# One mending branch in place of two ahead of the last unit's readings, in a mixture-of-experts tail

## The chip, the cores and the metric

The kernel runs on one core of a Trainium2 chip. The metric is device time in microseconds of one execution; lower is better. All numbers below come from runs of this program and from one profiled execution of it.

## What is computed

The program is a two-layer decoder on 8 sequences of 512 tokens and 256 channels, in float32. Only the end of the second layer matters here, the mixture of experts. Cut to that:

```python
tokens = hidden_states.reshape(-1, H)                  # 4096 x 256
topk_idx, topk_w = _route(tokens, ...)                 # 4 of 32 experts for each token
hidden_vals = silu(tokens @ gate_w) * (tokens @ up_w)  # for each expert
expert_out = hidden_vals @ down_w
mixed = (expert_out[topk_idx] * topk_w).sum(1)         # the 4 chosen experts' rows, weighted, added up
out = x + mixed + shared
```

## The kernel before, in words

The 4096 tokens are cut into 8 units of 512 tokens. A unit has 512 x 4 = 2048 assignments of a token to an expert, that is 16 tiles of 128. Routing sorts the assignments by expert and unit into a list in DRAM, `rows`, in pages of 128; each expert's share begins on a page of its own, so up to 32 pages (NE) are partly empty. In all there may be up to 160 pages (NS), and the program works through the first 136 (SURE, L31) without asking. How many pages are in use is known only on the chip.

**The main loop** is `pages_of(0, SURE, between)` (L1634, called at L1685), in an order written out by hand. For each page: SyncE (SP) reads the page (`fetch`, L1528), TensorE turns and multiplies it, VectorE (DVE) and ScalarE (ACT) evacuate, ACT weighs the result (L1574), and GpSimd (POOL) scatters the 128 result rows to their tokens' places in DRAM, `results`, by an indirect transfer (L944).

**The readings.** When a unit's pages are certainly done, its four tiles of 128 tokens are read back: `gather` (L1579) is a transfer of 512 KB on SP's queue into a buffer `z` of [128, 4, 256]; `add` (L1595) is three DVE instructions (L1602 one of 128x512, L1604 two of 128x256) that add the 4 rows of each token to `x`; `put` writes the sums to the output (L1612, two tiles at once on SP's queue, in the main loop; L1614, one tile on ACT's queue, after it). `finish` (L1619) puts these for units 0 to 6 between the pages.

**What may go wrong, and is mended.** A unit's readings are placed as if its pages ended at NE + 16 for each unit. Router sums say whether that was so. `experts` (L1352, run once before the main loop) makes two numbers in `used`: the rows in use, and how many of the first seven units ended later than `through` (L1373, L1374). After the main loop each of the five engines loads both numbers into registers (L1671) and branches on them:

- `rest(SURE)` (L1663): if more than 136 pages are in use, eight more pages, and within that branch the next eight, up to 160.
- `complete(range(7))` under `unready > 0` (L1702): if one of the first seven units was read too early, all of them are read, added and put once more.
- `complete([7])` (L1706), always: the last unit's four gathers, and per tile three additions and a put.

So the last unit's readings stand behind both branches.

**What a branch is in the built program.** Transfers on SP's and ACT's queues are counted in eight counters in turn (here HW0 to HW7), POOL's in eight others (SW0 to SW7), and each engine has a counter for its own instructions. After a branch the counters must stand the same whichever way it went. So the way around has, on each engine, one instruction for each counter that the engine's part of the branch would have moved: it waits until the counter has reached what was to come before the branch, and then adds what the branch would have added. On SP that is eight such instructions, in the order HW0 to HW7; on DVE and ACT one; on POOL four waits and one increment. Behind the second branch the first gather waits besides for the counters as the way around left them.

The last things SP does before the branches are two puts of unit 5 and two of unit 6 (L1612). The last put of unit 6 and the DVE addition it waits for were placed by the builder behind the first branch and ahead of the second.

Of the kernel before, what the change touches and what calls it, by code (L numbers as in the profile page):

```python
# [12 lines left out]
F32 = mybir.dt.float32  # L13
# [3 lines left out]
ALU = mybir.AluOpType  # L17
# [4 lines left out]
P = 128  # L22
B, S, H = 8, 512, 256
NT = S // P
# [6 lines left out]
SURE = 136  # L31
# [5 lines left out]
NE = 32  # L37
TOPK = 4
# [768 lines left out]
def _halves(x, u):  # L807

    h, p = divmod(u, B // 2)
    return [x[2 * p + r][:, 2 * h + t, :] for r in range(2) for t in range(2)]  # L810
# [54 lines left out]
def _l1(nc, tc, a, x, out, ident, mhalf, rows, results, filled, inputs, early):  # L865
# [12 lines left out]
    U = B  # L878
    seen = lambda u: 4 if u % 4 < 2 else 8
    with ExitStack() as ctx:  # L880
        pool = lambda name, bufs, **kw: ctx.enter_context(tc.tile_pool(name=name, bufs=bufs, **kw))
        routing, attention = ExitStack(), ExitStack()
        wp = routing.enter_context(tc.tile_pool(name="m_w", bufs=1, side="right"))
# [6 lines left out]
        vec = _Recorded(nc.vector)  # L890
# [13 lines left out]
            shared.append((gate, up, down))  # L904
        consts = {}
        for name, shape in (
            ("router_bias", [NE]), ("before", [16]), ("through", [U - 1])
        ):
            consts[name] = wp.tile([P, *shape], F32, tag=name, name=name)
            nc.sync.dma_start(consts[name], a[name].partition_broadcast(P))  # L910
        for name, width in (("earlier", P), ("pages", 2)):
            consts[name] = wp.tile([P, width], F32, tag=name, name=name)
            nc.sync.dma_start(consts[name], a[name])
        rb, before, earlier, pages, through = (
            consts[n] for n in ("router_bias", "before", "earlier", "pages", "through")
        )
# [15 lines left out]
        bounds = wp.tile([P, U, NE], F32, tag="bounds", name="bounds")  # L932
# [3 lines left out]
        def after(ins, others):  # L936
            info = mybir.DependencyInfo(mybir.DependencyClass.Sync, mybir.DependencyReason.DATA)
            for o in others:
                tc.add_manual_dep(ins.ins, o.ins.name, info, reason="rows of DRAM")
# [38 lines left out]
        def slow(name):  # L978

            return ps_d.tile([P, S], F32, tag="psd", name=name)  # L980
# [371 lines left out]
        def experts():  # L1352

            far = sb.tile([P, 2, B * NE], F32, tag="eq", name="far", bufs=1)
            vec.tensor_tensor(
                far,
                pages.unsqueeze(2).to_broadcast([P, 2, B * NE]),
                bounds.rearrange("p b e -> p (b e)").unsqueeze(1).to_broadcast([P, 2, B * NE]),
                ALU.is_ge,
            )  # L1360
            index = wp.tile([P, 2], F32, tag="index", name="index")
            vec.tensor_reduce(index, far, AX.X, ALU.add)
            ps = slow("pe")
            for c, width in enumerate((P, NS - P)):
                nc.tensor.matmul(
                    ps[:, c * P : c * P + width],
                    index[:, c : c + 1].to_broadcast([P, P]),
                    ident[:, :width],
                    start=True,
                    stop=True,  # L1370
                )
            vec.tensor_copy(used[:, 0:1], bounds[:, U - 1, NE - 1 : NE])
            late = wp.tile([P, U - 1], F32, tag="late", name="late")  # L1373
            vec.tensor_tensor(late, bounds[:, : U - 1, NE - 1], through, ALU.is_gt)  # L1374
            over = wp.tile([P, 1], F32, tag="over", name="over")
            vec.tensor_reduce(over, late, AX.X, ALU.add)
            vec.tensor_copy(used[:, 1:2], over)
            vec.tensor_copy(number, ps[:, :NS])
            vec.tensor_scalar(number, number, NE - 1, None, ALU.bitwise_and)
# [106 lines left out]
        for u in range(U):  # L1486
            t = start[u]
# [32 lines left out]
        tp = pool("m_t", 2)  # L1520
# [55 lines left out]

        z, sums_of = {}, {}

        def gather(u, t, sent):  # L1579

            h, p = divmod(u, 4)
            i = NT * (2 * p + t // 2) + 2 * h + t % 2
            z[u, t] = tp.tile([P, TOPK, H], F32, tag="z", name="z", bufs=5)
            ins = nc.sync.dma_start(  # L1584
                z[u, t].rearrange("p k c -> p (k c)"),
                results[i * P * TOPK : (i + 1) * P * TOPK, :].rearrange("(p k) c -> p (k c)", k=TOPK),
            )
            if sent:
                tc.declare_no_dep(
                    ins.ins, group="results", keep=[o.ins for o in sent], reason="later rows are none of its"  # L1590
                )
                tc.add_to_no_dep_group("gathers", ins.ins)
                after(ins, sent)

        def add(u, t, part):  # L1595

            w, x_t = z[u, t], _halves(x, u)[t]
            if t == 0 and part == 0:
                sums_of[u] = tp.tile([P, NT, H], F32, tag="sums", name="sums", bufs=3)
            to = sums_of[u][:, t, :]  # L1600
            if part == 0:
                nc.vector.tensor_tensor(w[:, :2, :], w[:, :2, :], w[:, 2:, :], ALU.add)  # L1602
            else:
                nc.vector.tensor_tensor(to, x_t if part == 1 else to, w[:, part - 1, :], ALU.add)  # L1604

        def put(u, t, queue=nc.sync):

            h, p = divmod(u, 4)
            to = out.rearrange("b (t p) c -> b p t c", p=P)
            if isinstance(t, tuple):  # L1610
                (r,) = t
                nc.sync.dma_start(to[2 * p + r, :, 2 * h : 2 * h + 2, :], sums_of[u][:, 2 * r : 2 * r + 2, :])  # L1612
            else:
                queue.dma_start(to[2 * p + t // 2, :, 2 * h + t % 2, :], sums_of[u][:, t, :])  # L1614
# [48 lines left out]
        def rest(s):  # L1663

            with tc.If(filled_rows > s * P):
                with tc.manual_schedule():
                    pages_of(s, s + 8, lambda _: None)
                if s + 8 < NS:
                    rest(s + 8)
# [11 lines left out]
            max_val=NS * P,  # L1681
            skip_runtime_bounds_check_because="the rows of the pages in use",
        )
        with tc.manual_schedule():
            pages_of(0, SURE, between)  # L1685
            for s in sorted(beside):
                for f in beside[s]:
                    f()
        rest(SURE)

        def complete(units):

            last = [(u, t) for u in units for t in range(NT)]
            for n in range(-4, len(last)):
                if n >= 0:
                    for part in range(3):
                        add(*last[n], part)
                    put(*last[n], nc.scalar)
                if n + 4 < len(last):
                    gather(*last[n + 4], None)  # L1700

        with tc.If(unready > 0):  # L1702
            with tc.manual_schedule():
                complete(range(B - 1))
        with tc.manual_schedule():
            complete([B - 1])  # L1706


@with_exitstack
# [30 lines left out]
def _buckets(r):  # L1740

    d = np.abs(r)
    d = np.where(d < 32, 31, d)
    far = np.ceil(np.log(d / 32) / np.log(127 / 32) * 31 - 1e-6) + 32
    return np.where(d <= 32, d, far * np.sign(r)).astype(np.int64)


def _constants():
    onehot = np.zeros((2, P, W), np.float32)
    j = np.arange(W - 1)  # L1750
    for t, r in enumerate((127 - j, j - 127)):
        place = 64 - _buckets(-r) if t else 64 + _buckets(r)
        onehot[t, np.clip(place, 0, 127), j] += 1.0
        onehot[t, np.where(r > 0, 127, 0), j] -= 1.0
    m = np.arange(P)
    tail = np.zeros((P, 2), np.float32)
    for e, t, value in ((HD, 0, 1.0), (HD + 1, 0, -1.0), (HD + 2, 1, -SCALE), (HD + 3, 1, SCALE)):
        tail[m % 32 == e, t] = value
    i = np.arange(4)
    heads = np.zeros((P, NK, 32), np.float32)  # L1760
    for k in range(NK):
        heads[m, k, NH // NK * k + m // HD] = 1.0

    tiles = np.arange(NB).reshape(B // 2, 2, 2, 2).transpose(2, 0, 1, 3).reshape(NB)
    before = (i[None, :] < i[:, None]).astype(np.float32).reshape(16)
    return {
        "onehot": onehot,
        "tail": tail,
        "later": np.tril(np.ones((P, P), np.float32), -1),
        "before": before,  # L1770
        "heads": heads,
        "through": (P * (NE + S * TOPK // P * np.arange(B - 1))).astype(np.float32),
        "pages": (P * (m[:, None] + P * np.arange(2))).astype(np.float32),
        "earlier": np.triu(np.ones((P, P), np.float32), 1),
        "dest": (
            (P * tiles[None, :, None] + m[:, None, None]) * TOPK + np.arange(TOPK)
        ).astype(np.int32),
        "spare": (NTOK * TOPK + P * np.arange(NS)[None, :] + m[:, None]).astype(np.int32),
    }
# [20 lines left out]
def _layout(v):  # L1800
# [26 lines left out]
        "supT": v["L1_ffn_shared_up_w"].T,  # L1827
        "sdownT": v["L1_ffn_shared_down_w"].T,
        **_constants(),
    }  # L1830

# [16 lines left out]
```

## Time and profile before

| | us |
|---|---|
| median of 3 runs (lowest, highest) | 2007.52 (2006.33, 2018.69) |
| the profiled execution's own time | 2012.53 |
| its span, first to last instruction | 2010.7 |

TensorE, the busiest engine, has its last matmul at 1989.1 us of the span. What follows is the tail that the change touches. In it PE, ACT and POOL compute nothing after 1991.8 us; SP, DVE and the transfers are what is left.

How to read the profile: times are from the start of the span. An engine's name with a q (SPq, DVEq) means an instruction that only its sequencer executes: a wait or a count (EVENT_SEMAPHORE), a branch (COMPARE_BRANCH), a register load (TENSOR_LOAD) or the issue of a transfer (DMA_DIRECT2D). A row of EVENT_SEMAPHORE begins when what it waits for has come. The answer for one source line gives, for each kind of instruction on each engine, its count, its shortest, median and longest duration in ns, and the start of the first and the last.

### The profile page before, as it was taken

The page shows a single profiled execution, that of the slowest core. Times are in us where ns is not written, and L with a number is a line of the kernel's source. Part 1 is how long each engine was busy: PE and PEld are TensorE (multiplying, and loading weights), DVE is VectorE, ACT ScalarE, POOL GpSimd, SP SyncE. Part 2 cuts the span into 40 slices and gives each one's busy share as a digit, 9 for nine tenths or more (in the row PEclk, how much of TensorE's full clock was granted, in tenths as well). Part 3 has the DMA queues.
Part 4 walks back from the last instruction along what each step waited for, and adds up shares of the span by engine and source line. Part 5 has one row for each costly group of instructions (what it writes and reads, how often), then busy time and mean ns, then how long its engine had stood idle before and what let it go on. Part 6 is the DMA issues. An engine that isn't in the chain of part 4 may idle for free. (4 is left out here: it accounts for less than half of the span.)

```text
span 2010.7 us, 48841 instructions
## 1 busy us (share of the span) xinstructions
PE 1887.2 (94%) x17824; PEld 1292.1 (64%) x17824; DVE 1369.8 (68%) x3675; ACT 1087.6 (54%) x2320; POOL 1095.5 (54%) x1294
## 2 busy tenths in 40 slices
PE   7999999999999999999999999989899886899995
PEld 4666676666667666666666666646556544488884
DVE  4677777777777777776777555346887687356666
ACT  3777677777777777777762221235444333144442
POOL 4666786867868678676783110100444444455553
PEclk9999999999999999999999999999999998799998
DMA  8999999999999999999993434910111112747887
GB/s 294 318 310 288 293 297 300 299 298 304 294 304 311 295 306 296 303 283 297 298 311 116 141 121 139 131 21 0 44 44 47 52 49 89 289 150 232 249 259 242
DMA packets 383060, 438.07 MB, mean 218 GB/s; under 512 B 42849, under 2 KB 364385, under 8 KB 382305
## 3 DMA queue, kind: packets, MB, share of 16 engines
q1 hardware_dynamic: 368608, 398.17, 64.7%
q0 software_dynamic: 12672, 35.14, 4.8%
q8 instruction: 146, 2.39, 0.5%
q10 hardware_dynamic: 1536, 1.57, 0.2%
q14 instruction: 98, 0.79, 0.1%
HBM read 235.75 MB, written 199.05 MB: 216 GB/s over the span
## 5 line engine op out<-in xcount | busy, mean ns | idle before, releaser
L448 DVE CUSTOM_DVE_ANT_0 e<-sc,winc 128x512 f32<-128x512 f32 x512 | 333.2, 689 | 280.2 <-PE sc L434 156.6
L451 ACT ACTIVATE e<-e,low 128x512 f32<-128x512 f32 x512 | 365.6, 715 | 96.8 <-DVE low L448 95.7
L372 ACT COPY strip<-pa 128x512 f32<-128x512 f32 x512 | 275.2, 591 | 129.0 <-POOL winc L402 59.2
L375 POOL TENSOR_TENSOR own<-aside,strip 128x512 f32<-128x512 f32 x256 | 269.0, 1051 | 124.9 <-ACT strip L372 108.2
L465 DVE COPY et<-et_ps 128x512 f32<-128x512 f32 x512 | 328.4, 683 | 0.8 <-PE et_ps L462 0.8
L422 PE MATMUL sc<-sm,sm 32*128 32x256 f32 (+3 forms) x1792 | 310.0, 436 | 1.0 <-DVE low L448 0.8
L365 PE MATMUL pa<-pos,sm 32*128 32x256 f32 x2048 | 291.9, 401 | 0.1
L944 POOL DMA_INDIRECT rows<-pay,slot x128 | 148.7, 1162 | 210.7 <-issue 156.8
L402 POOL TENSOR_TENSOR winp<-winp,own 128x256 f32<-128x256 f32 x256 | 187.7, 733 | 98.1 <-DMA winp<-shift 76.2
L422 PEld LDWEIGHTS sc<-sm,sm 32*128 32x128 f32 x1792 | 164.5, 184 | 98.0 <-DVE et L465 35.3
L434 PE MATMUL sc<-ident,winp 128*128 128x128 f32 x1280 | 203.2, 286 | 24.7 <-DMA winp<-shift 24.3
L402 POOL TENSOR_TENSOR winc<-winc,own 128x256 f32<-128x256 f32 x256 | 187.2, 731 | 57.9 <-DMA winc<-shift 46.4
L434 PEld LDWEIGHTS sc<-ident,winp 128*128 128x128 f32 x1280 | 137.1, 142 | 102.4 <-issue 58.3
L944 POOL DMA_INDIRECT results<-y,r x136 | 133.3, 980 | 105.0 <-ACT y L1574 54.7
L462 PE MATMUL et_ps<-ident,e 64*128 64x64 f32 x4096 | 184.4, 230 | 1.1 <-DVE et L465 1.1
L365 PEld LDWEIGHTS pa<-pos,sm 32*128 32x128 f32 x2048 | 176.1, 185 | 10.9 <-ACT strip L372 3.9
L59 POOL TENSOR_TENSOR rstd<-var,mhalf 128x2 f32<-128x2 f32 (+1 forms) x56 | 47.2, 844 | 243.4 <-DVE var L57 235.0
L462 PEld LDWEIGHTS et_ps<-ident,e 64*128 64x128 f32 x4096 | 149.1, 140 | 44.2 <-issue 22.2
L474 PE MATMUL ctx_ps<-et,v 128*32 128x128 f32 x4096 | 167.7, 282 | 0.5 <-DVE et L465 0.5
L1554 PE MATMUL pge<-store,rT 128*128 x544 | 141.3, 382 | 3.1 <-DVE rT L1548 1.4
L739 ACT ACTIVATE hT<-ph,b 128x512 f32<-128x512 f32 x64 | 44.0, 687 | 165.6 <-PE ph L736 165.6
L175 PE MATMUL pq<-xnT,wqk 128*128 128x512 f32 x256 | 132.7, 643 | 0.7 <-PE pv L157 0.7
(227 smaller groups left out, 3200.6 us busy)
## 6 DMA issues: line engine op xcount, KB each, us to landing
shift<-strip SPq DMA_DIRECT2D x256, 510.0 KB
winp<-shift SPq DMA_DIRECT2D x128, 384.0 KB
winc<-shift SPq DMA_DIRECT2D x128, 384.0 KB
winp<-shift SPq DMA_DIRECT2D x128, 256.0 KB
winc<-shift SPq DMA_DIRECT2D x128, 256.0 KB
rows<-empty SPq DMA_DIRECT2D x8, 2640.0 KB
r<-rows SPq DMA_DIRECT2D x136, 132.0 KB
z<-results SPq DMA_DIRECT2D x32, 512.0 KB
```

Of the source, the lines that this page charges most:

```text
L365: nc.tensor.matmul(pa[:, t * W : (t + 1) * W], src[rs, i * P : (i + 1) * P], pos[rs, g, :], start=True, stop=True)
L372: nc.scalar.copy(st[:, 2 * j : 2 * j + 2, :].rearrange("p t w -> p (t w)"), pas[j])
L375: nc.gpsimd.tensor_tensor(own, aside.unsqueeze(2).to_broadcast([P, 2, 2, P]), st[:, :, W - 1 : W].rearrange("p (j t) o -> p t j o", t=2).t ...
L402: nc.gpsimd.tensor_tensor(dst, dst, own[:, t], ALU.add)
L422: nc.tensor.matmul(sc[:, c0:c1], s[side_][rs, cut : cut + P], s[2 + side_][rs, c0:c1], start=c0 == 0, stop=False, skip_group_check=True,)
L434: nc.tensor.matmul(sc[:, m * P : (m + 1) * P], wins[n + 2 * (m - i)][1][:, j, (i - m + 1) * P : (i - m + 2) * P], ident, start=False, stop ...
L448: nc.vector.tensor_tensor_reduce(e, sc, wins[n][0][:, j, :], 1.0, -LOW, ALU.add, ALU.min, low)
L451: nc.scalar.activation(e, e, AF.Exp, bias=low, scale=-1.0, accum_out=totals[b, g // 2][:, i, r : r + 1])
L462: nc.tensor.transpose(bank[:, c : c + 64], e[rs, m * P : (m + 1) * P], ident[rs, rs])
L465: nc.vector.tensor_copy(et[:, f].rearrange("p j m q -> p (j m q)"), bank)
L474: nc.tensor.matmul(ctx_ps[32 * r : 32 * r + 32, i * P : (i + 1) * P], vs[b % 2][:, m, g % 2, g // 2 * 4 + r, :], et[:, :, m, :], start=m = ...
L944: ins = nc.gpsimd.indirect_dma_start(to, bass.IndirectOffsetOnAxis(ap=index, axis=0), source, None, bounds_check=last)
```

## The change

The last unit is treated like the others. Its four gathers are issued in the main loop's own sequence, right behind the last pages and unit 6's puts, as if 136 pages were enough. Whether that was so is added to `late`, which now has 8 columns; `through` has 8 values, none above 128 x 136. One branch on `unready > 0` holds everything that mends: the further pages, and all eight units' gathers (into the four buffers that the last unit has), with additions and puts of the first seven. Behind the branch the last unit's additions and puts follow in any case.

```diff
-            ("router_bias", [NE]), ("before", [16]), ("through", [U - 1])
+            ("router_bias", [NE]), ("before", [16]), ("through", [U])
...
-            late = wp.tile([P, U - 1], F32, tag="late", name="late")
-            vec.tensor_tensor(late, bounds[:, : U - 1, NE - 1], through, ALU.is_gt)
+            late = wp.tile([P, U], F32, tag="late", name="late")
+            vec.tensor_tensor(late, bounds[:, :, NE - 1], through, ALU.is_gt)
...
-        def gather(u, t, sent):
+        def gather(u, t, sent, to=None):
...
-            z[u, t] = tp.tile([P, TOPK, H], F32, tag="z", name="z", bufs=5)
+            z[u, t] = tp.tile([P, TOPK, H], F32, tag="z", name="z", bufs=5) if to is None else to
...
+        def summed_up(u, t):
+
+            for part in range(3):
+                add(u, t, part)
+            put(u, t, nc.scalar)
+
         with tc.manual_schedule():
             pages_of(0, SURE, between)
             for s in sorted(beside):
                 for f in beside[s]:
                     f()
-        rest(SURE)
-
-        def complete(units):
-
-            last = [(u, t) for u in units for t in range(NT)]
-            for n in range(-4, len(last)):
-                if n >= 0:
-                    for part in range(3):
-                        add(*last[n], part)
-                    put(*last[n], nc.scalar)
-                if n + 4 < len(last):
-                    gather(*last[n + 4], None)
-
+            for t in range(NT):
+                gather(B - 1, t, None)
         with tc.If(unready > 0):
+            rest(SURE)
             with tc.manual_schedule():
-                complete(range(B - 1))
+                for u in range(B):
+                    for t in range(NT):
+                        gather(u, t, None, z[B - 1, t])
+                    for t in range(NT if u < B - 1 else 0):
+                        summed_up(u, t)
         with tc.manual_schedule():
-            complete([B - 1])
+            for t in range(NT):
+                summed_up(B - 1, t)
...
-        "through": (P * (NE + S * TOPK // P * np.arange(B - 1))).astype(np.float32),
+        "through": (P * np.minimum(NE + S * TOPK // P * np.arange(B), SURE)).astype(np.float32),
```

In the built program SP's order at the end becomes: the four puts of units 5 and 6; the four gathers of unit 7, counted in HW6, HW7, HW0 and HW1, the first of which waits for the last scatter's counter SW7; the load of `used`; the branch; on the way around it the eight counters HW0 to HW7, each waited for at its value behind the gathers. DVE's order becomes: unit 6's last addition; the load; the branch; its own counter; then the twelve additions, where the four tiles' first instructions wait for HW7 and HW6, for HW1, for HW3 and for HW5, each (but HW6) as the way around or the branch has moved it. No instruction ahead of unit 6's last addition and put changes its place on any engine.

## The prediction

> **What bounds the kernel now.** I read the page first, then the chain of waits, then the tail line by line. TensorE is busy for 94% of the span, but nothing that the change touches lies beside it: the chain that ends last is wholly in the tail.
>
> ```profile
> span 2010.7 us, 48841 instructions
> PE 1887.2 (94%) x17824; PEld 1292.1 (64%) x17824; DVE 1369.8 (68%) x3675; ACT 1087.6 (54%) x2320; POOL 1095.5 (54%) x1294
> ```
>
> The chain of waits, in order of time (start, duration, what):
>
> ```profile
> 1997.95 3.54 DMA z<-results
> ...
> 2001.72 0.70 DVE z L1602
> ...
> 2007.46 0.43 DVE sums L1604
> ```
>
> The last unit's first gather is issued at 1997.95 us and lands 3.54 us later, at 2001.49. The first addition starts at 2001.72, and the twelve run without a gap that a transfer makes until 2007.89: 6.17 us. From 2007.89 to the end at 2010.7 there are a put of 128 KB and the closing of the program; both stay. So the question is only when the first addition starts.
>
> Three answers about SP say what holds the gathers back. By line: the load of `used`, the first branch, the second branch (count, durations in ns, first and last start).
>
> ```profile
> L1671 SPq TENSOR_LOAD <-used x1: 1157/1157/1157, 1990.4 to 1990.4; - x1
> ...
> L1671 DVEq TENSOR_LOAD <-used x1: 934/934/934, 1992.1 to 1992.1; - x1
> ```
>
> ```profile
> L1665 SPq EVENT_SEMAPHORE  x8: 17/17/17, 1992.1 to 1994.5; - x8
> L1665 SPq COMPARE_BRANCH  x1: 50/50/50, 1991.6 to 1991.6; - x1
> ```
>
> ```profile
> L1702 SPq EVENT_SEMAPHORE  x8: 17/17/17, 1995.3 to 1997.6; - x8
> L1702 SPq COMPARE_BRANCH  x1: 45/45/45, 1995.1 to 1995.1; - x1
> ```
>
> And the timeline of SP between them:
>
> ```profile
> 1994.66 0.37 SPq L1612 DMA_DIRECT2D out<-sums  x1
> 1997.95 1.84 SPq L1584 DMA_DIRECT2D z<-results  x4
> ```
>
> The reader is to see that a branch instruction itself takes 0.05 us, and that the eight counts of a way around take 2.4 and 2.3 us, because they wait for transfers under way. In the trace's single rows the first way stands until 1994.34, when the third put has landed. The last put is then issued at 1994.66, and the second way stands until 1997.49 for that same put's landing (1997.47). The timeline of DVE shows the addition that this put waits for, held back by the first branch:
>
> ```profile
> 1992.02 0.42 DVE L1604 TENSOR_TENSOR sums<-x,z 128x256 f32<-128x256 f32 x1
> 1993.84 0.42 DVE L1604 TENSOR_TENSOR sums<-sums,z 128x256 f32<-128x256 f32 x1 [1.39 <-DVEq L1665]
> ```
>
> The last scatter, which the gathers do need, is seen to have landed by POOL's wait of the first branch at 1994.87, and the fourth gather by SP's closing wait at 2005.36 (the last row of each answer):
>
> ```profile
> L1665 POOLq EVENT_SEMAPHORE  x1: 43/43/43, 1994.9 to 1994.9; - x1
> ```
>
> ```profile
> L1844 SPq EVENT_SEMAPHORE  x2: 28/28/28, 2004.1 to 2005.4; - x2
> ```
>
> Neither branch is entered: the answers by line count 136 page readings (L1528) and 32 gathers (L1584, 7 x 4 in the loop and the last 4).
>
> **The change part by part.**
>
> *The wider `through` and `late`.* One column more in one DVE instruction and one small load, at 1742 us; the neighbouring one-column conversions there take 0.14 and 0.15 us, so under 0.02 us. I take nothing; whole cost in the open, 0.02.
>
> *Unit 6's last addition and put.* The addition no longer stands behind the first branch: it follows the one at 1992.02 by 0.46 (as 2002.44 is followed by 2002.90) and ends at 1992.91. The put is issued at 1992.93 instead of 1994.66, which passes no other transfer on SP's queue.
>
> *The four gathers, moved ahead of the load and the branch.* They wait for the last scatter alone: the first goes at 1994.88 instead of 1997.95, 3.07 us sooner. Their landings are a matter of bandwidth: from issue, 3.54 us to the first and 2005.34 - 1997.95 = 7.39 to the fourth, 1.28 apart (2 MB at 402 to 447 GB/s in that stretch). So they land at 1998.42, 1999.70, 2000.98 and 2002.27.
>
> *The one branch, now between the gathers and the additions.* SP has issued the gathers by 1996.7, loads `used` (1.16), branches and reaches its first count 0.46 later (1991.61 to 1992.07 before): 1998.4. Here the cost is hidden by the gathers' flight. But the counts are not free of them: the gathers are counted in HW6, HW7, HW0 and HW1, and the way around waits for each of these at its value behind the gathers. HW0 stands until the third gather has landed (2000.98), HW1 until the fourth (2002.27). The first addition waits for HW7, which comes last of the eight: six counts after HW1 at 0.07 us (0.06 to 0.09 in the rows before) make 2002.71; 0.14 for DVE's own wait and start, as before between its last wait and its work, make 2002.85. Before, the first addition needed the first gather; now it needs all four. That is 2002.85 - 2001.72 = +1.13 us.
>
> So of the 3.07 us gained at the issue, 3.85 (7.39 - 3.54) go to the wait for the fourth landing and some 0.35 to the counts. What queues behind the waiting SP is nothing but the closing; behind DVE's wait are all twelve additions, and ACT's puts behind these. The additions stay back to back, for all data are there: 6.17 us.
>
> *Unit 6's last put beside the last scatters.* Before, it moved after the scatters had landed; now its 256 KB start about 1 us after 1992.93, in the scatters' last microsecond. Nothing makes the last scatter earlier than 1994.85, so below, nothing. Above: the third put, which did run beside scatters, had its bulk in at 1992.80 and its last part at 1994.32, 1.5 us more. The overlap is a third of that one's; I take 0.3 and keep 0 to 1.5.
>
> *POOL, ACT, PE* lose one branch each, POOL also a 1.22 us increment of its counters. They have nothing left to do but wait: ACT's first put came at 2003.36 with its branch done by 1990.7. Nothing.
>
> **Sum:** +1.13 + 0.3 = +1.4 us. The profiled execution's own time would go from 2012.53 to 2013.9 us. It lies 5.0 above the median of the runs, 2007.52, so the difference is carried over: **2008.9 us**. The likeliest case alone reaches from +0.8 to +2.9 (2008.3 to 2010.4).
>
> [...] The row of the branch comes first: 0.05 us for the instruction, but 1995.09 to 1997.95 from the second branch to the gather. [...] The second row: SP needs 0.46 us from its branch to the next instruction, while PE's answer for the same line has this:
>
> ```profile
> L1665 PEldq COMPARE_BRANCH  x1: 4420/4420/4420, 1989.7 to 1989.7; - x1
> ```
>
> [...]
>
> **The rivals.**
>
> *A. The additions start with the first landing,* as the readings' early issue suggests. SP's counts would end by 1998.4 + 8 x 0.07 = 1999.0, the additions run from 1999.1 to 2005.27 (the fourth tile starts at 2003.7, after its landing): 2.6 us less, 2004.9. Against it stands that HW0 and HW1 are waited for ahead of HW7. For it: only that a landing could be counted differently than I read it.
>
> *B. SP reaches its counts late.* With PE's 4.42 in place of 0.46 it would be there at 2002.4, and all eight counts would follow: 0.25 above my forecast. From 4.3 us on each microsecond counts in full; at 6.5 us, half more than the longest seen, the end is at +3.7, 2011.2.
>
> *C. The mending branch is entered, slower by over 1%.* One mechanism: more than 136 pages in use. Price: 32 gathers at 1.28 = 41 us, with eight more pages at the loop's 1.63 us = 13, at least 54 us, 2061. It decides from the 137th page on. Against it: 136 page readings in the trace of before, where the same number would have led into the first branch.
>
> *D. Nothing moves:* +-0.5 us, if the put's overlap makes nothing and the transfers are quicker by what the tighter issue of the gathers (their extra waits go) may give, at most 0.2 x 3. 2007.5.
>
> **How the numbers follow.** Forecast 0.70, A 0.08, B 0.12, C 0.02, D 0.08. The predicted time is the first's. A measurement of this kernel can tell about 1% (20 us) from no change, and the whole tail after the last matmul is 21.6 us long: a gain of over 1% isn't to be had. Range: from A, 2004.9, less the 1.2 by which the lowest run lay under the median, some 2004; to B's 2011.2 and as much again above it, 2013. Faster by over 1% 0.01 (the runs' own spread), within 1% 0.96, slower by over 1% 0.03 (C and that spread).
>
> **What would show it.** In the profile after: unit 6's last addition at 1992.5 and put at 1992.9; gathers issued near 1994.9 to 1995.2; SP's counts of the one branch beginning near 1998.4 and ending only just after the fourth landing, near 2002.7 to 2003; the first of the twelve additions 0.1 to 0.2 later, with its wait put down to SP or to the gathers, and 6.2 us for the twelve. An addition before the fourth landing refutes the forecast for A; counts that begin after 2002.3 are B; more than 136 pages read are C; a last scatter much after 1995.2 says that the put's overlap was mis-sized.

## The result, and the profile after

| | before | after | ratio, 95% interval |
|---|---|---|---|
| median of 20 runs each, us | 2009.15 | 2017.45 | 1.0034 [1.0021, 1.0048] |
| again, beside the first experiments, us | 2018.13 (35 runs) | 2021.17 (12 runs) | 1.0018 [0.9994, 1.0041] |

The ratios are worked out from the single runs; the medians alone differ by 8.3 and 3.0 us. By the ratios the kernel became slower by 6.8 us (4.2 to 9.6) in the first comparison and by 3.6 (-1.2 to 8.3, which takes in no change) in the second: within 1% as forecast, in the direction forecast, and some 2.5 to 5 times the +1.4 us of the sum. The time itself, 2017.45, lies above the range (2004 to 2013). Of the miss of 8.5 us, 1.6 is that the kernel before ran at 2009.15 here instead of 2007.52.

The profiled execution of after took 2010.57 us, the lowest of its 20 runs. Its span is even shorter than that of before, so the two spans can't be subtracted:

```profile
span 2008.8 us, 48814 instructions
...
PE 1883.1 (94%) x17824; PEld 1290.8 (64%) x17824; DVE 1367.2 (68%) x3675; ACT 1087.8 (54%) x2320; POOL 1097.2 (55%) x1294
```

The main part before the tail varies by more than the whole tail's change: the last scatter is issued at 1990.69 in before, and at 1986.09 and 1996.28 in the two profiles of after. So the tails are compared, counted from that issue, which is called L from here on. "Flight" is the time from the first of the last unit's four gathers' issue to the fourth landing.

| us after L | before | after | after, second profile |
|---|---|---|---|
| last scatter landed | 4.16 | 3.98 | 3.91 |
| unit 6's last put issued | 3.98 | 2.25 | 2.25 |
| first gather issued | 7.26 | 3.99 | 3.93 |
| second gather's issue takes | 0.33 | 1.02 | 1.07 |
| the four landings | 10.80, 12.08, 13.37, 14.65 | 7.69, 9.40, 11.07, 12.34 | 8.10, 11.00, 12.24, 13.48 |
| flight | 7.39 | 8.35 | 9.55 |
| first addition | 11.03 | 13.30 | 14.44 |
| last put issued | 17.23 | 19.50 | 20.65 |
| end of the span | 20.06 | 22.69 | 23.84 |

So the tail became 2.6 and 3.8 us longer. The profile shows where. The end of the chain of waits of after (start, duration, what):

```profile
1998.92 0.05 DVEq L1602
1998.97 0.42 issue
1999.39 0.70 DVE z L1602
...
2005.14 0.42 DVE sums L1604
```

No gather stands in it any more: in before it held 3.54 us of `DMA z<-results`, here it begins with DVE's wait. The timeline of DVE names what released the first addition (in brackets the idle time and its end):

```profile
1987.89 0.42 DVE L1604 TENSOR_TENSOR sums<-sums,z 128x256 f32<-128x256 f32 x1
1999.39 0.69 DVE L1602 TENSOR_TENSOR z<-z 128x512 f32<-128x512 f32 x1 [11.08 <-SPq L1697]
```

It is SP's way around the branch, 11 us after unit 6's last addition, and not a gather. The answer for the branch's line, of after (count, shortest, median and longest in ns, first and last start):

```profile
L1697 SPq EVENT_SEMAPHORE  x8: 17/17/17, 1997.2 to 1998.9; - x8
...
L1697 PEldq COMPARE_BRANCH  x1: 4172/4172/4172, 1985.1 to 1985.1; - x1
...
L1697 POOLq INC_SWDGE_SEM  x1: 1222/1222/1222, 1990.2 to 1990.2; - x1
L1697 SPq COMPARE_BRANCH  x1: 50/50/50, 1993.3 to 1993.3; - x1
```

SP branches at 1993.32, but its first count goes through at 1997.18, with the third landing (L + 11.07), and the second at 1998.45, with the fourth (L + 12.34); six more follow 0.07 apart. That is the forecast's mechanism. What it did not contain is in the answer for the gathers' line, and in that for the DMA queues between 1990.0 and 1991.2, while the second gather was being issued (queue and kind: packets, MB, share of the 16 DMA engines):

```profile
L1584 SPq DMA_DIRECT2D z<-results x4: 338/427/1021, 1990.1 to 1992.0; - x4
```

```profile
q1 hardware_dynamic: 35, 0.05, 15.6%
q8 instruction: 1, 0.02, 5.0%
q14 instruction: 1, 0.01, 2.5%
```

One issue takes 1.02 us where 0.33 to 0.43 is usual for these four (up to 0.48 in before's main loop), and beside it an instruction fetch of 16 KB and one of 8 KB are under way. The fourth landing comes 0.96 us later after the first issue than in before.

### The profile page after: what moved, and what is told of

It reads as the page before. It is cut to its first block, busy times and chain, and to the rows that moved or that the text cites. A ratio compares the mean times of both kernels' runs of the same rounds, so it can differ in the third digit from the quotient of the medians.

```text
span 2008.8 us, 48814 instructions
## 1 busy us (share of the span) xinstructions
PE 1883.1 (94%) x17824; PEld 1290.8 (64%) x17824; DVE 1367.2 (68%) x3675; ACT 1087.8 (54%) x2320; POOL 1097.2 (55%) x1294
```

## The experiments

Each was timed against the kernel before on the same chip, four of them together, in the order in which they stand here. The diffs show the main lines of each edit. Before's median was 2018.13, 2027.80 and 2010.94 us beside the three groups, so a median is compared only within its group. "Tail" is the end of the span after L; before's is 20.06, after's 22.69 and 23.84.

### Only the wider constant

```diff
-("through", [U - 1])
+("through", [U])
-            late = wp.tile([P, U - 1], F32, tag="late", name="late")
+            late = wp.tile([P, U], F32, tag="late", name="late")
```

(with the eight values; all the rest as before)

> Before, with only the constants and the comparison of the change: through and late have 8 columns, both branches stay where they were. Tail theory (the whole difference lies behind the last scatter, where the changed kernel's profile is 2.6 us longer: 22.7 us from the last scatter's issue to the end in place of 20.1): no difference from before, within 1 us, and 20.1 us from the last scatter to the end. Place theory (some 4 us of the measured 6.8 come from the main part, because the constant of 32 bytes in place of 28 shifts what lies behind it in DRAM): 4 us slower than before with an unchanged tail.

Measured: ratio 0.9997 [0.9980, 1.0014], tail 19.98. The place theory falls: its 4 us would be 1.0020, outside the interval, and the wider constant costs nothing that shows.

### The changed kernel again

> The changed kernel once more, for a second profile of the same program. Tail theory: 2.6 us slower than before if its first profile is typical, and 22.7 us from the last scatter's issue to the end; if the measured 6.8 us are all tail, a profile with a tail of up to 27 us must turn up. Place theory: 6.8 us slower with a tail near 22.7 us. In both the first addition starts only after the fourth gather's landing.

Measured: ratio 1.0018 [0.9994, 1.0041], tail 23.84. The mechanism is the same (first count at the third landing, first addition 0.96 after the fourth). The flight is longer still, 9.55. A tail near 27 us, which would hold the whole 6.8, did not turn up.

### The mending last

```diff
+        with tc.manual_schedule():
+            for t in range(NT):
+                summed_up(B - 1, t)
         with tc.If(unready > 0):
...
-                    for t in range(NT if u < B - 1 else 0):
+                    for t in range(NT):
                         summed_up(u, t)
-        with tc.manual_schedule():
-            for t in range(NT):
-                summed_up(B - 1, t)
```

> The change with its branch moved behind the last unit's additions and puts (the branch then reads, adds and puts all eight units again). The additions then need only their own gather. Tail theory: the first addition starts 0.2 us after the first landing, some 7.9 us after the last scatter's issue in place of 13.3 in the changed kernel and 11.0 before; the closing pays some 0.6 us for the branch; 2.5 us faster than before. Place theory: the same tail, but 4 us more in the main part, so 1.5 us slower than before.

Measured: ratio 1.0002 [0.9985, 1.0019], tail 20.77. The timeline of DVE of this kernel:

```profile
1999.40 0.69 DVE L1602 TENSOR_TENSOR z<-z 128x512 f32<-128x512 f32 x1 [6.23 <-DMA z<-results]
...
2002.14 0.69 DVE L1602 TENSOR_TENSOR z<-z 128x512 f32<-128x512 f32 x1 [1.13 <-DMA z<-results]
```

With the branch behind them the additions begin at L + 8.45, at the first landing, and wait for gathers again. So the order of the branch and the additions is what holds them in after. But little of it reaches the end, which is 0.7 later than before's and not 2.5 us earlier as expected: the second addition stands 1.13 us, since the flight is 9.85, and the end comes 4.89 after the last put (2.83 before); ACT's load and branch now follow that put, and SP's closing waits for DVE's way around:

```profile
SPq L1845 <- DVEq L1700: 1.0, 1, 1.0
```

DVE's row there comes at L + 19.28, 2.9 us after its branch.

### No mending at all

The branch and what it holds are left out (work that the kernel would need if pages were late); the built program then has no load of `used` in its trace either.

> The change without any branch: the mending is left out altogether, the rest is as in the changed kernel. The floor of the tail. Tail theory: first addition 7.9 us after the last scatter's issue, about 17 us from there to the end, 3.1 us faster than before. Place theory: 4 us more, 0.9 us slower than before.

Measured: ratio 0.9976 [0.9953, 0.9998], tail 16.43. That is the floor of this order, 3.6 below before. The gathers' line again, the last four of them, and the DMA queues while they were issued (2001.1 to 2003):

```profile
L1584 SPq DMA_DIRECT2D z<-results x4: 339/423/430, 2001.2 to 2002.5; - x4
```

```profile
q1 hardware_dynamic: 147, 0.26, 46.4%
```

No issue is long, no fetch is there, and the flight is 7.55. So the long flights of after came with the branch. Three things that the branch brings lay beside the gathers: POOL's increment of its counter (1.22 us), the register load (0.68 us on SP), and the instruction fetches (0.95 us for the one of 16 KB, 0.47 for the one of 8; all as in after). The next four part them.

### No scatters in the mending branch

```diff
-                    pages_of(s, s + 8, lambda _: None)
+                    pages_of(s, s + 8, lambda _: None, False)
```

(`False`: the result isn't scattered)

> The changed kernel, but the further pages in the mending branch don't scatter their results (work that is left out), so POOL has no counter to bring up on the way around the branch: its 1.22 us increment, and the 16 KB instruction fetch beside it, should be gone. All else of the branch stays. L is the issue of the last scatter. In the changed kernel the second gather's issue takes 1.02 us (0.42 without a branch) just while that increment runs, and from the first gather's issue to the fourth landing it takes 8.35 and 9.55 us in its two profiles, where it took 7.4 to 7.6 in the three kernels without the coincidence. Increment theory: POOL's increment does both. Then the second issue is back at 0.42, the fourth landing 7.4 to 7.6 after the first issue, the first addition at L + 12.5 (4.0 + 7.55 + the 0.96 from the fourth landing to the first addition) and the end at L + 21.9. Load theory: the register load and the branch beside the gathers thin the transfers. Then flight and tail stay at 8.3 or more and L + 22.7 or more, though the second issue may shorten.

Measured: ratio 1.0022 [1.0001, 1.0043], second issue 1.46, flight 8.52, tail 22.55. The increment is gone and the long issue is not. The gathers' line, the branch's line and the queues from 2012.6 to 2014.2:

```profile
L1585 SPq DMA_DIRECT2D z<-results x4: 339/427/1463, 2012.6 to 2015.0; - x4
```

```profile
L1698 PEldq EVENT_SEMAPHORE  x2: 51/51/51, 2012.0 to 2012.1; - x2
L1698 PEldq COMPARE_BRANCH  x1: 4252/4252/4252, 2007.6 to 2007.6; - x1
```

```profile
q1 hardware_dynamic: 22, 0.07, 46.0%
q8 instruction: 1, 0.02, 5.7%
```

The increment theory falls, and so does the belief that the 16 KB fetch was POOL's: it stayed where it was, about half a microsecond after TensorE's way around.

### No further pages in the mending branch

```diff
         with tc.If(unready > 0):
-            rest(SURE)
             with tc.manual_schedule():
```

> The changed kernel without the further pages in the mending branch (work that is left out): no increment on POOL, and every engine jumps over far less code. Increment theory: the same as without the scatters, second issue 0.42, flight 7.4 to 7.6, end at L + 21.9. A fetch theory (what the engines jump over must be followed by a fetch of instructions, which delays them and the transfers): better than without the scatters alone; the time from the fourth landing to the first addition, 0.96 in the changed kernel, falls to about 0.5, end at L + 21.4. Load theory: flight stays at 8.3 or more, end at L + 22.7 or more.

Measured: ratio 0.9987 [0.9969, 1.0005], second issue 0.70, flight 8.26, fourth landing to first addition 0.60, tail 21.49. TensorE has no pages to jump over (its branch takes 0.25 us), and of the fetches beside the gathers' issue only one of 8 KB is left. The 16 KB one is gone and with it most of the issue's delay: this and the run before speak for the fetch.

### The load in the main loop

The five engines load `used` beside page 104.

```diff
         def between(s):
+
+            if s == 104:
+                read_used()
```

> The changed kernel, but the five engines load the two numbers of used in the main loop, beside page 104, instead of between the last gathers and the branch. Increment theory: POOL's increment still falls on the second gather's issue (1.0 to 1.3 us), the flight stays at 8.3 to 9.9, the counts wait for the landings as before, end at L + 22.7 to L + 23.8. Load theory: the flight falls to 7.4 to 7.6, end at L + 21.9.

Measured: ratio 1.0020 [0.9996, 1.0045], second issue 1.41, flight 9.86, tail 23.88. The load theory falls.

### The mending last, with the early load

> The last unit's additions and puts stand ahead of the mending branch, which mends all eight units and comes last (end at L + 20.77 when the numbers are loaded there, 4.89 after the last put), and the numbers are loaded in the main loop, beside page 104. Increment theory: first addition at L + 8.4, last put at L + 15.9, the closing 3.2 after it instead of 4.89: end at L + 19.1, 1.0 below the kernel before. Load theory: the flight falls from 9.85 to 7.5 too, last put at L + 13.7, end at L + 16.9.

Measured: ratio 0.9992 [0.9969, 1.0015], second issue 1.52, flight 8.85, last put L + 14.83, tail 19.19. The end is as expected, but in a different way: the last put came 1.1 sooner, from a shorter flight, and the closing took 4.36, hardly less than 4.89. The load is not what makes that closing long. By the rows DVE's way around is no longer what SP waits for here, but the last put lands 2.1 us after its issue (1.7 before), and SP's last counts and its closing waits then follow one by one, from L + 16.94 to 18.28.

### TensorE's branch held back

```diff
+            pt = ps_t.tile([P, S], F32, tag="pst", name="pth")
+            nc.tensor.transpose(pt[:, :P], z[B - 1, 1][:, 0, :P], ident)
         with tc.If(unready > 0):
```

> The changed kernel with one idle transpose on TensorE, ahead of its load and branch, that reads the second gather's tile: so TensorE's branch, and the 16 KB instruction fetch 0.4 to 0.5 us after its way around, come behind the second gather's landing instead of beside its issue. Fetch theory (that fetch, not POOL's increment and not the register loads, holds up the second gather's issue and thins the transfers): second issue 0.42 to 0.70, the fourth landing 7.6 to 8.0 after the first gather's issue, first addition at L + 12.8, end at L + 22.2 or less. Rival (the longer flight has another cause, or is chance): flight still 8.3 or more, end at L + 22.7 or more, even if the second issue is short again.

Measured: ratio 1.0010 [0.9996, 1.0024], second issue 0.54, flight 8.28, first addition L + 12.49, tail 21.89. The gathers' line, the queues while they were issued (1987.8 to 1989.4), TensorE's way around, and the queues from 1994.8 to 1996:

```profile
L1584 SPq DMA_DIRECT2D z<-results x4: 339/426/538, 1987.8 to 1989.3; - x4
```

```profile
q1 hardware_dynamic: 145, 0.17, 52.9%
q14 instruction: 1, 0.01, 1.8%
```

```profile
L1699 PEldq COMPARE_BRANCH  x1: 3922/3922/3922, 1993.3 to 1993.3; - x1
```

```profile
q8 instruction: 1, 0.02, 5.0%
q1 hardware_dynamic: 7, 0.02, 4.3%
```

The 16 KB fetches went where TensorE's branch went (L + 10.69 and 13.79), POOL's increment stayed (L + 3.7), and the second issue shrank from 1.02 or more to 0.54. So the fetch is TensorE's, and it is what held the issue. The flight did not come down to 7.6 to 8.0: the third landing is still 1.05 us later than the 1.28 behind the second, with two fetches of 8 KB shortly before (L + 9.13, 10.32). That part of the expectation failed. The last view shows what the remainder looks like: at the end of the flight the gathers' packets of 4 KB go one after the other for 0.95 us, with none beside them. Why these come so late is not settled.

### One branch, ahead of the gathers

```diff
         with tc.If(unready > 0):
+            rest(SURE)
             with tc.manual_schedule():
                 complete(range(B - 1))
```

(before's order; the pages and the seven units are mended in one branch ahead of the last unit's gathers)

> One branch for all that mends, as in the changed kernel, but ahead of the last unit's gathers, as the two branches stood. Counter theory (a way around costs what it waits for, the transfers under way at that point): unit 6's put goes at L + 2.25 and lands near L + 5.1, POOL's increment ends at L + 5.3, SP's counts are through near L + 5.4 and the gathers go from L + 5.5, 1.8 sooner than with two branches; first addition at L + 9.3, end at L + 18.3. Rival (the price lies in branches and loads, not in what stands under way): two branches less one save 0.1 to 0.5, the gathers go from L + 6.8 or later, end at L + 19.5 or later.

Measured: ratio 1.0005 [0.9987, 1.0023], first gather L + 5.97, second issue 0.33, flight 7.36, first addition L + 9.72, tail 18.75. The answer for the branch's line on SP:

```profile
L1700 SPq EVENT_SEMAPHORE  x8: 17/17/17, 1992.7 to 1993.2; - x8
L1700 SPq COMPARE_BRANCH  x1: 50/50/50, 1992.2 to 1992.2; - x1
```

Eight counts in 0.5 us, where they took 2.4 and 2.3 in before: here nothing under way was left to wait for. Putting the two branches into one, without moving it, is worth 1.3 us of tail, less than the 1.8 expected. SP's waits name the reason:

```profile
SPq L1584 <- DVEq L1700: 0.7, 1, 0.7
```

The first gather waits for DVE's counter, which DVE's own way around brings up at L + 5.92, 3.2 us after its branch at L + 2.75. DVE's last addition had counted at L + 2.23, so no wait that the profile shows holds DVE there; the reason for its delay is open.

### The mending's transfers on POOL

```diff
-gather(u, t, None, z[B - 1, t])
+gather(u, t, None, z[B - 1, t], nc.gpsimd)
-                        summed_up(u, t)
+                        summed_up(u, t, nc.gpsimd)
-                    pages_of(s, s + 8, lambda _: None)
+                    pages_of(s, s + 8, lambda _: None, nc.gpsimd)
```

(the last argument is the queue; the branch stands where after has it)

> The changed kernel, but every transfer inside the mending branch is issued by POOL, so that the way around moves none of the eight counters that the last unit's gathers are counted in; SP has nothing to wait for there. Counter theory: the additions begin with the first landing, first addition at L + 7.9 to L + 8.6, last put at L + 14.0 to L + 15.2 (the fetch beside the second gather's issue stays), end 2.8 to 3.2 later, L + 16.8 to L + 18.4. Rival (the way around as such, or the branch, holds the additions): first addition at L + 10 or later, end at L + 20 or later.

Measured: ratio 1.0002 [0.9982, 1.0021], tail 18.71. The timeline of DVE:

```profile
1996.05 0.69 DVE L1602 TENSOR_TENSOR z<-z 128x512 f32<-128x512 f32 x1 [6.12 <-DMA z<-results]
...
1998.89 0.69 DVE L1602 TENSOR_TENSOR z<-z 128x512 f32<-128x512 f32 x1 [1.23 <-DMA z<-results]
```

The branch is where it is in after, and the additions begin at L + 8.40 with the first landing. So the branch itself holds nothing; the counters that its way around waits for do. The second issue took 1.56 and the flight 9.79, and so the last put came at L + 15.92, 0.7 beyond the upper end of what was expected, and the end 0.3 beyond it.

### Both together

> The changed kernel with both: the mending transfers on POOL, and TensorE's branch held behind the second gather's landing. Counter and fetch theories: second issue 0.42 to 0.70, flight 7.6 to 8.0, first addition at L + 7.5 to L + 7.9, last put at L + 13.7 to L + 14.1, end at L + 16.5 to L + 17.2, within 0.8 of the kernel without any mending (L + 16.43) and 2.9 to 3.6 below the kernel before. If the fetch does nothing: as with the transfers on POOL alone.

Measured: 2006.20 against 2010.94, ratio 0.9983 [0.9965, 1.0000], second issue 0.42 (the third 0.68, beside a fetch of 8 KB), flight 8.17, first addition L + 7.47, last put L + 13.88, tail 17.42. The lines of TensorE and POOL, and of DVE's first addition:

```profile
L1699 POOLq INC_SWDGE_SEM  x1: 1227/1227/1227, 1992.4 to 1992.4; - x1
...
L1699 PEldq COMPARE_BRANCH  x1: 4132/4132/4132, 1997.9 to 1997.9; - x1
```

```profile
1996.09 0.69 DVE L1602 TENSOR_TENSOR z<-z 128x512 f32<-128x512 f32 x1 [5.25 <-DMA z<-results]
```

The tail is 2.6 us shorter than before's and 5.3 to 6.4 shorter than after's, with all the mending kept; the flight is 0.2 longer and the end 0.2 later than expected. In time it is 3.4 us less than before (0 to 7.0): the best complete version of the study, at the edge of what this measurement can tell.

### What the fourteen profiles say of the flight

The last column is counted from the gathers' packets of 4 KB, of which some 16 are under way in the middle of a flight: until how long after the first issue 12 or more are.

| 16 KB fetch of TensorE beside the gathers' issue | flights, us | 12 or more packets until, us |
|---|---|---|
| no, gathers behind the branches or no branch (before, the wider constant, one branch ahead; no mending) | 7.39, 7.45, 7.36; 7.55 | 6.69, 6.73, 6.66; 6.84 |
| no, but a branch behind the gathers (no further pages, TensorE held, both together) | 8.26, 8.28, 8.17 | 6.83, 6.71, 6.82 |
| yes (after twice, mending last, no scatters, early load, mending last with the early load, on POOL) | 8.35, 9.55, 9.85, 8.52, 9.86, 8.85, 9.79 | 7.38, 7.75, 7.99, 7.56, 7.56, 7.65, 7.51 |

The flights alone part the second group from the third by only 0.07 us, and the two profiles of one kernel differ by 1.2. The packets part them clearly. Without the 16 KB fetch the bulk of them runs until 6.66 to 6.84 us after the first issue, whether a branch stands behind the gathers or not; with it the bulk runs 0.5 us longer at least, since there are stretches in it in which fewer packets end (in after 14 in the half microsecond from L + 8.5, where about 50 is usual). That is the fetch's part. The rest is a straggling end: from the last column to the last packet it takes 0.3 to 0.4 us in the first group, 0.9 to 1.1 in the second and 0.6 to 2.0 in the third. It comes with a branch behind the gathers, with and without the 16 KB fetch, and no run shows its cause.

That the fetch holds the issue is shown closely: in all seven profiles of the third group the second issue ends 0.37 to 0.39 us after the fetch ends, while the fetch's own length varies from 0.95 to 1.75 us. In before and after all 146 fetches on q8 are of 16 KB, and those on q14 in the tail are of 8 KB. That the ones on q8 are TensorE's is shown by the runs that held its branch back (they went along, to L + 10.69 and 13.79) or left it no pages to jump over (none beside the gathers' issue). Whose those on q14 are, and in what way a fetch of one engine holds up the issue of another's transfer, no run shows.

## Why the prediction was right in kind and wrong in size

**Unit 6's put**, predicted at L + 2.24, was issued at 2.25. Its overlap with the last scatters (+0.3) cost nothing: they landed at 3.98 and 3.91, against 4.16.

**The gathers' issue**, predicted 3.07 us sooner, came 3.27 sooner. What stood ahead of the gathers on SP in before were the load of `used` (1.16 us) and the two branches' counts (2.4 and 2.3); the branch instructions themselves took 0.05 each.

**The one branch's counts.** Right, and the centre of the forecast: HW0 went through with the third landing, HW1 with the fourth, the other six 0.07 apart, and the first addition needed all four. The mending on POOL shows it by an edit: without these counters the additions begin with the first landing.

**The flight.** Here the forecast failed. It took 7.39 us from a trace in which the gathers were issued when the branches' fetches were over (before's last of 16 KB ran from L + 4.28 to 5.30, its last of 8 KB began at 6.06, the first gather went at 7.26), and called the landings "a matter of bandwidth"; and it took "POOL, ACT, PE" at "Nothing", because they had nothing left to compute. Moving the gathers 3.3 us forward moved their issue onto TensorE's fetch. The flight became 8.35 and 9.55: +0.96 and +2.16. By the packets 0.7 and 1.1 us of that are the later end of the bulk, which goes with the fetch, and the rest is the straggling end, whose cause is open. Holding TensorE back took the first part away (6.71 against before's 6.69) and left the second: 8.28, and 8.17 with the mending on POOL.

**From the fourth landing to the first addition** the forecast had 0.58 us (six counts and 0.14); 0.96 was measured, since DVE stands 0.42 us between its last wait and its work. It did not without the further pages (0.60), nor with TensorE held (0.60, where DVE has one wait more). The **closing** was 0.36 longer too: near its end two of SP's counts stand 0.39 us apart instead of 0.07, in after (both profiles), with the early load and with TensorE held, whose closings take 3.2 us instead of 2.8. In these profiles a fetch of 8 KB begins 0.6 to 0.7 us after such a stand of SP, and in all but the last of them after that of DVE. No run tests what these stands are.

**The sum, as it should have been:** first gather -3.27, flight to the fourth landing in place of the first landing 8.35 - 3.54 = +4.81, landing to addition 0.96 - 0.23 = +0.73, closing 3.19 - 2.83 = +0.36: +2.63 us, the tail's difference. With the other profile's 9.55 it is +3.78. Against the forecast's +1.43 the parts are: flight +0.96, landing to addition +0.38, closing +0.36, put -0.3, issue -0.2.

**What stays open.** The first comparison gives 4.2 to 9.6 us, the second -1.2 to 8.3; the profiled tails give 2.6 and 3.8. The tail thus fits the second measurement, and falls short of the first by 0.4 at least. In eleven of the twelve experiments the tail's difference from before lies inside the interval of the time (without the further pages it lies 0.4 us above it), and over the twelve the time's difference is on average 0.1 us below the tail's. So nothing but the first comparison points to a cost outside the tail; whether its rest is scatter, the runs don't say.

**The rivals.** A (additions from the first landing) didn't come: the first addition stood until the fourth. B carried TensorE's long branch (4.42 us) over to SP, and SP was not late (where it has no counts to wait for, as with the mending on POOL, its next row comes 0.18 us after the branch); but behind TensorE's branch came a fetch of TensorE's, and it held up SP's issue of the second gather. C: 136 page readings and 32 gathers, the branch wasn't entered. D: the tail moved by more than its 0.5. On the counters all experiments agree. Of the longer flight the runs show the part that goes with TensorE's fetch beside the issue; the straggling end remains without that fetch (flights of 8.17 to 8.28 against 7.36 to 7.55), and its cause is open.

## What to carry to other kernels

A skipped branch cost here what its way around waited for: SP's eight counts took 2.4 and 2.3 us with puts under way (before), 0.5 with nothing left to wait for (one branch ahead), and stood until the fourth landing behind the gathers (after); TensorE and DVE stood up to 4.9 and 3.6 us at a branch, in which no wait shows. So before a branch is moved behind transfers, ask in which counters those are counted and whether the branch would move these; with the mending's transfers on another queue the first addition came at L + 8.40 instead of 13.30. And when a transfer is moved, look at what every engine does at the new time, its branches and instruction fetches too: an engine that has nothing left to compute is not an engine that does nothing. A duration read from the old place need not hold at the new one: the flight of 7.39 us became 8.35 and 9.55.

## What the runs showed of the hardware that was not expected

- The issue of a 512 KB transfer on SP's queue took 1.02 to 1.56 us instead of 0.33 to 0.43 in all seven profiles in which a 16 KB instruction fetch of TensorE ran beside it (the fetch itself took 0.95 to 1.75), and the longest issue 0.54 to 0.70 in three with fetches of 8 KB alone. A fetch of 8 KB need not lengthen it: with one branch ahead one ran beside the second issue, which took 0.33.
- TensorE's branch instruction stood 3.9 to 4.4 us in before, after, without scatters, with TensorE held and with both together, at L - 1 as at L + 9, and 4.75 and 4.90 in the two kernels with the early load; it stood 0.25 where there were no pages to jump over. On SP, DVE, ACT and POOL the same branch took 0.05 to 0.07. But DVE's next row, for which the profile shows no wait, came 2.2 and 2.3 us behind it at the second branch of before and of the wider constant, and 2.9 to 3.6 in five kernels (mending last with and without the early load, one branch ahead, on POOL, both together), where it was 0.6 in the others.
- The load of the same two numbers took SP 1.08 to 1.33 us ahead of the gathers (before, one branch ahead, the wider constant) and 0.67 to 0.68 behind them.
